# Four conv layers in one kernel: linear attention as one pipeline of 12 items, its aggregation sums in SBUF

## Chip, cores and metric

The kernel runs on one core of a Trainium2 chip. The metric is the device time of one execution in microseconds; the kernel before takes 8581.61 us, the median of three runs (8575.27 to 8585.84). Five engines work side by side, each through its own queue in order: PE (matmul), DVE (elementwise and reductions), ACT (activation and copies), POOL (here: indirect gathers) and SP (plain DMAs).

## The reference, cut to what matters

Input x is (4, 256, 64, 64) in fp32. Four layers follow, each `x = x + layer(groupnorm(x))`.

```python
# layer 0: 1x1 conv, depthwise 3x3 -> offsets and mask, deformable sampling, then SE and a 256-1024-256 feed-forward
# layer 1: linear attention
qkv = relu(conv1x1(x, qkv_w) * qkv_bn_scale + qkv_bn_bias)        # 768 channels
agg = depthwise5x5(qkv, agg_dw_w) + agg_dw_b
agg = agg * agg_pw_w + agg_pw_b                                   # per channel
t = concat([qkv, agg]).reshape(B, -1, 3 * 8, H * W)
q, k, v = split(t, 3, axis=2);  q, k = relu(q), relu(k)
vk = einsum('bhdn,bhen->bhde', v, k)
out = einsum('bhde,bhen->bhdn', vk, q)
denom = einsum('bhe,bhen->bhn', k.sum(-1), q)
out = relu(conv1x1(out / (denom + eps), proj_w) * s + b)
# layer 2: 3x3 conv with binarised weights
# layer 3: non-local attention: softmax(theta(x)^T phi(maxpool(x))) g(maxpool(x)), a 1x1 conv, + x
```

## The kernel before, in words

Each image (n = 0 to 3) goes through generators that yield a cost after each few instructions: `convolve` and `shifts` (layer 0 up to the sampling tables), `sample` (the deformable sampling), `feedforward`, `layer1`, `layer2` and `layer3`. All intermediate images lie in DRAM; blocks of 512 pixels x 256 channels are loaded again by each generator.

`run` puts generators side by side with `beside(steps, number, *works)`: for each step of the leading generator the others are advanced in proportion to their declared total cost, within a share of the stage (lo to hi). The stages are: convolve(0); sample(0) beside convolve(1 to 3) and the shifts; sample(1) beside the weights of layer 2 (`binarise`), feed(0) and linear(0); sample(2) beside feed(1), linear(1) and second(0); sample(3) beside feed(2), linear(2) and second(1); feed(3), linear(3) and second(2); second(3). Here `linear` is layer1 and `second` is layer2, then layer3. Feed has the first fifth of a stage, linear and second the rest. In the stages with `sample` the queues of PE, DVE, ACT and POOL hold the instructions in the order in which the generators issue them (`ordered`); elsewhere a scheduler orders them.

`sample` (L195 on counts rounds of 14 pixels x 9 points). A round issues four indirect DMAs on POOL (L561) that fetch 128 rows of 1 KB each into `g`, addressed by indices in `sl` in SBUF; PE multiplies them with the weights `wm` (L568) into a half of the bank `acc`, ACT copies it out (L573), PE transposes (L578), ACT spreads (L593), and per block PE projects (L601) and DVE adds (L605). `wm` is made by DVE for four rounds at a time (L552), from `con` and `sl`, both in SBUF. `g` has seven buffers, `wm` two.

`layer1` runs three passes over the image: for t = 0, 1 the tiles k and v, then the tiles q. In each pass `rows` (L727) computes two 128-channel tiles of qkv per block (L741), ACT applies scale, bias and relu, and copies the rows into padded tiles of 20 x 68 (16 rows and a border, three buffers for each of the two tiles). As soon as 16 rows and their border are there, the chunk is handed out, and `aggregate` (L759) forms the 5 x 5 depthwise sum with `depthwise` (L169): the first tap by L178 `tensor_scalar`, 24 taps by L176 `scalar_tensor_tensor`, acc = pad * w + acc, over 128 x 1024 elements each. The accumulator `agg` lies in PSUM, in one buffer of two banks; ACT then copies it to SBUF (L764), with relu for k and q. The same `depthwise`, with nine taps, is used by `offsets` in layer 0.

What comes of a chunk is put on a list, `later`, from which each `step` takes one entry: for k and v the transposes, the copy `kt` and the products into `vk` (`outer`); for q the denominators (`dens`, DVE reciprocal), per head `num`, `rden` and the multiplication (L844), and the projection (`output`). At the end of each k, v pass the list is emptied and the sums are masked (L814 to L817).

PSUM's eight banks: `agg` two, `vk`, `acc` and `dp` one each, and three that everything else shares (`mm`), handed out in turn by `ps()`.

```python
self.mm = e(tc.tile_pool(name="mm", bufs=3, space=PSUM))
...
acc = self.ps1.tile([P, 16, W], F32, name="agg", tag="agg")
```

`layer3` forms th, ph and gt from x5, then for each 128 pixels two score banks `s` (L984), the maximum on DVE (L985, L986), the exponential on ACT (L991), eight transposes (L999, L1000), the product with gt (L1004) and the division (L1005); per block a 1x1 conv (L1010), the residual (L1011, L1012) and the store.

Of the kernel before, what the change touches and what calls it, by code (L numbers as in the profile page):

```python
# [9 lines left out]
F32 = mybir.dt.float32  # L10
# [23 lines left out]
TY, TX = H + 2, W + 3  # L34
SLOPE = 0.01
# [5 lines left out]
LINEAR = 1130  # L41
SECOND = 631
# [27 lines left out]
class Net:  # L70
    def __init__(self, ctx, tc, a, out):
        self.tc, self.nc, self.a, self.out = tc, tc.nc, a, out
        e = ctx.enter_context
        self.cp = e(tc.tile_pool(name="const", bufs=1, side="left"))
        self.gp = e(tc.tile_pool(name="gather", bufs=2, side="left"))
        self.sp2 = e(tc.tile_pool(name="samp", bufs=2, side="left"))
        self.ps1 = e(tc.tile_pool(name="ps1", bufs=1, space=PSUM))
        self.mm = e(tc.tile_pool(name="mm", bufs=3, space=PSUM))
        self.dp = e(tc.tile_pool(name="scratch", bufs=1, space=DRAM))


    def ps(self, name="ps"):
        return self.mm.tile([P, 512], F32, name=name, tag="mm")
# [85 lines left out]
    def depthwise(self, acc, src, w, k, rows, cols, r0, bias=None, step=lambda cost: cost):  # L169

        nc = self.nc
        for t in range(k * k):
# [8 lines left out]
            if t % 3 == 2 or t == k * k - 1:  # L181
                yield step(3.9)

# [251 lines left out]
    def offsets(self, n, c, y, mw, bp, used):  # L435
# [3 lines left out]
        for k in range(KT):  # L439
            acc = self.ps1.tile([P, 16, W], F32, name="agg", tag="agg")  # L440
# [76 lines left out]
    def sample(self, n, ssum):  # L517
# [4 lines left out]
        nc, sp = self.nc, self.sp2  # L522
# [177 lines left out]
    def layer1(self, n, st, st2):  # L700
# [3 lines left out]
        with tc.tile_pool(name=f"la{n}", bufs=1, side="right") as sp, \  # L704
# [14 lines left out]
            later = []  # L719

            def step(cost):

                if later:
                    later.pop(0)()
                return cost

            def rows(tiles, seen):  # L727


                new = lambda c: [self.padded(bp, 1, 20, 2, c, f"pad{i}", bufs=3) for i in range(2)]  # L730
                pads = {0: new(0)}
                for b in range(NB):
                    c, h = divmod(b, 2)
                    x = self.block(bp, self.x3_d[n], b, "xr")
                    if h and c + 1 < NCH:
                        pads[c + 1] = new(c + 1)
                    got = []
                    for i, t in enumerate(tiles):
                        ps = self.ps()
                        for k in range(KT):  # L740
                            nc.tensor.matmul(ps, qw[:, k, t * P:(t + 1) * P], x[:, k], start=k == 0, stop=k == KT - 1)  # L741
                        bn = {"bias": qb[:, t:t + 1], "scale": self.vec("qkv_s", t)}
                        dst = {j: p[i][:, 0] for j, p in pads.items()}
                        if seen:
                            v = bp.tile([P, 512], F32, name="v", tag=f"v{i}")
                            added = {} if i else {"accum_out": seen[0][:, b:b + 1]}
                            nc.scalar.activation(v, ps, AF.Relu, **bn, **added)
                            self.spread(dst, rw(v), b, 2)
                            got.append(v)
                        else:  # L750
                            self.spread(dst, None, b, 2, lambda own: nc.scalar.activation(own, rw(ps), AF.Relu, **bn))  # L751
                        yield step(3)
                    if seen:
                        seen[1](b, got)
                    if b and not h:
                        yield c - 1, [p[:, 0] for p in pads.pop(c - 1)]
                yield NCH - 1, [p[:, 0] for p in pads[NCH - 1]]

            def aggregate(pd, i, name, func, **more):  # L759

                acc = self.ps1.tile([P, 16, W], F32, name="agg", tag="agg")
                yield from self.depthwise(acc, pd, self.w5[:, i], 5, 16, W, 0, bias=self.b5[:, i:i + 1], step=step)
                v = bp.tile([P, 16, W], F32, name=name, tag="ag", bufs=3)
                nc.scalar.activation(v, acc, func, **more)  # L764
                yield step(2)
                return v

            for t in range(2):
                ks = sp.tile([P, 2, NB], F32, name=f"ks{t}")
                sums = {}  # L770

                sums[0] = self.ps1.tile([P, 2, P], F32, name="vk", tag="vk")

                def outer(kind, kv, vv, first, last):

                    at = [slice(i, i + 256) for i in range(0, kv.shape[1], 256)]
                    kts = []

                    def turned(cs):
                        pt = self.ps("pt").rearrange("p (s j c) -> p s j c", s=2, j=2)  # L780
                        for j in range(2):
                            nc.tensor.transpose(pt[:, 0, j], kv[:, cs][:, j * P:(j + 1) * P], self.ident)
                            nc.tensor.transpose(pt[:, 1, j], vv[:, cs][:, j * P:(j + 1) * P], self.ident)
                        kts.append(bp.tile([P, 2, 2, P], F32, name="kt", tag="kt", bufs=4))
                        nc.scalar.copy(kts[-1], pt)

                    def added(i):
# [384 lines left out]
```

## Time and profile before

The profiled execution took 8571.0 us, 8569.0 us of it the span of the trace; the mean granted TensorE clock was 0.842.

| | busy us | share of span | instructions |
|---|---|---|---|
| PE | 6457.6 | 75% | 35252 |
| DVE | 5259.4 | 61% | 6319 |
| ACT | 2008.5 | 23% | 4711 |
| POOL | 4583.8 | 53% | 4694 |

The costliest groups are the gathers (L561, 4688 of 978 ns) and the aggregation taps (L176, 2560 of 1288 ns). The chain that ended last is mostly PE (25% of the span) and DVE (12%). POOL works until 6594 us and not at all after. A busy share is a mean over stages with different limits, so the stages have to be looked at one by one; and idle time of an engine that doesn't set the end costs nothing.

### The profile page before, as it was taken

Reading aid. Unit: us, or ns where it says so; the run is one execution under the profiler, and the core shown is the slowest. Engines: PE = TensorE matmul, PEld = TensorE weight load, DVE = VectorE, ACT = ScalarE, POOL = GpSimd, SP = SyncE. Lnnn points to the kernel's source line nnn. Section 1 sums busy time; section 2 is a strip of 40 time slices with the busy share of each in tenths; the row PEclk is TensorE's granted clock in tenths of the full one; section 3 lists DMA queues with packets and bytes.
Section 4 is the critical chain, followed back from the end, with each engine's and each line's share of the span. In section 5 each row is a group of like instructions: output and inputs, shape, how many; then the busy total and the mean of one; then the engine's idle time right before and its main releaser. Section 6 shows DMA issues by size and latency. Waiting matters only on the chain. (4 is left out here: it accounts for less than half of the span.)

```text
span 8569.0 us, 92678 instructions
## 1 busy us (share of the span) xinstructions
PE 6457.6 (75%) x35252; PEld 3474.4 (41%) x35252; DVE 5259.4 (61%) x6319; ACT 2008.5 (23%) x4711; POOL 4583.8 (53%) x4694
## 2 busy tenths in 40 slices
PE   4666666587666668999667789896678988567887
PEld 2333433344333323444444444444444444343445
DVE  5555554635878782378877723878776278988113
ACT  1111111122221122222232222223322221222113
POOL 1777777777777776777775567777654000000000
PEclk8676767798666789999888999997888999788999
DMA  6475655565444445555443354544432211110210
GB/s 172 141 197 150 179 167 160 158 189 164 123 122 119 140 127 151 148 146 148 147 128 108 113 166 147 151 140 149 126 112 86 93 60 37 47 37 35 58 58 30
DMA packets 819964, 1054.93 MB, mean 123 GB/s; under 512 B 464320, under 2 KB 524864, under 8 KB 817984
## 3 DMA queue, kind: packets, MB, share of 16 engines
q0 software_dynamic: 225024, 614.77, 24.5%
q1 hardware_dynamic: 594496, 434.25, 17.4%
q8 instruction: 279, 4.57, 0.2%
q14 instruction: 165, 1.35, 0.0%
HBM read 880.72 MB, written 167.90 MB: 122 GB/s over the span
## 5 line engine op out<-in xcount | busy, mean ns | idle before, releaser
L561 POOL DMA_INDIRECT g<-tab,sl x4688 | 4583.1, 978 | 2010.6 <-issue 1484.2
L176 DVE SCALAR_TENSOR_TENSOR agg<-pad,vec,agg 128x1024 f32<-128x1024 f32 x2560 | 3296.0, 1288 | 69.7
L568 PE MATMUL acc<-g,wm 128*32 128x128 f32 x18752 | 1330.8, 320 | 1210.5 <-ACT at L573 628.7
L568 PEld LDWEIGHTS acc<-g,wm 128*32 128x32 f32 x18752 | 644.8, 121 | 1938.1 <-DMA g<-tab,sl 835.7
L905 PE MATMUL ps<-xp,w 128*128 128x512 f32 x2304 | 1066.3, 610 | 81.7 <-DVE xp L889 53.1
L593 ACT COPY dT<-dp 64x112 f32<-64x112 f32 x1176 | 286.6, 244 | 1627.6 <-PE dp L578 1132.6
L905 PEld LDWEIGHTS ps<-xp,w 128*128 128x128 f32 x2304 | 427.7, 193 | 568.7 <-issue 537.1
L552 DVE TENSOR_TENSOR wm<-con,sl 128x1024 f32<-128x1024 f32 (+1 forms) x296 | 358.3, 1211 | 358.6 <-PE acc L568 339.6
L686 PE MATMUL ps<-x2f,f 128*128 128x512 f32 x1024 | 476.6, 615 | 4.0 <-ACT f L677 4.0
L693 PE MATMUL ps<-hm,f 128*128 128x512 f32 x1024 | 453.6, 597 | 0.0
L167 DVE SCALAR_TENSOR_TENSOR hm<-ps,vec,lk 128x512 f32<-128x512 f32 x256 | 192.3, 751 | 417.3 <-ACT lk L166 416.2
L741 PE MATMUL ps<-xr,qw 128*128 128x512 f32 x768 | 417.6, 674 | 9.7 <-ACT pad L751 1.7
L999 PE MATMUL pt<-ident,pe 128*128 128x128 f32 x1024 | 194.2, 339 | 228.6 <-ACT pe L991 226.6
L991 ACT ACTIVATE pe<-s,mx 128x512 f32<-128x512 f32 x256 | 173.6, 683 | 714.3 <-DVE mx L986 714.3
L573 ACT COPY at<-acc 128x256 f32<-128x256 f32 (+1 forms) x588 | 218.3, 371 | 481.4 <-PE acc L568 471.8
L1004 PE MATMUL ps<-gt,pT 128*128 128x128 f32 x2048 | 320.5, 321 | 4.9 <-ACT pT L1000 2.8
L1004 PEld LDWEIGHTS ps<-gt,pT 128*128 128x128 f32 x2048 | 298.6, 231 | 50.4 <-issue 19.0
L601 PE MATMUL po<-dT,ow 128*128 128x224 f32 (+1 forms) x1216 | 293.6, 392 | 19.7 <-DVE yb L605 12.9
L166 ACT ACTIVATE lk<-ps,low 128x512 f32<-128x512 f32 x256 | 175.9, 687 | 557.0 <-PE ps L686 557.0
L694 DVE TENSOR_TENSOR xyf<-xyf,ps 128x512 f32<-128x512 f32 x64 | 44.0, 688 | 409.6 <-PE ps L693 409.6
L686 PEld LDWEIGHTS ps<-x2f,f 128*128 128x128 f32 x1024 | 192.0, 194 | 232.8 <-issue 222.4
L693 PEld LDWEIGHTS ps<-hm,f 128*128 128x128 f32 x1024 | 190.6, 190 | 231.5 <-issue 231.1
(226 smaller groups left out, 7037.4 us busy)
## 6 DMA issues: line engine op xcount, KB each, us to landing
x<-x SPq DMA_DIRECT2D x160, 512.0 KB
g<-tab,sl POOLq DMA_INDIRECT x4688
xr<-x SPq DMA_DIRECT2D x96, 512.0 KB
x<-in_x SPq DMA_DIRECT2D x64, 512.0 KB
tab<-xo SPq DMA_DIRECT2D x512, 64.0 KB
y<-yc SPq DMA_DIRECT2D x32, 512.0 KB
x2f<-x SPq DMA_DIRECT2D x32, 512.0 KB
xyf<-x SPq DMA_DIRECT2D x32, 512.0 KB
```

The source lines that it names most:

```text
L176: nc.vector.scalar_tensor_tensor(acc, s, wt, acc, ALU.mult, ALU.add)
L552: nc.vector.tensor_tensor(wm[:, 0:nu], self.con("own").unsqueeze(1).unsqueeze(1).to_broadcast(sh), sl[:, r:r + nu, G:].unsqueeze(3).to_bro ...
L561: nc.gpsimd.indirect_dma_start(out=g[:, i, :], out_offset=None, in_=table, in_offset=bass.IndirectOffsetOnAxis(ap=sl.bitcast(I32)[:, r, i: ...
L568: nc.tensor.matmul(acc[32 * i:32 * i + 32, :], wm[:, r4, 4 * i + 2 * x:4 * i + 2 * x + 2, :], g[:, i, x * P:(x + 1) * P], start=x == 0, st ...
L573: nc.scalar.copy(at[u].rearrange("p v c -> p (v c)")[:, 0:nu * P], acc[:, 0:nu * P])
L593: nc.scalar.copy(dT[b][hs, :, q0:q0 + m * (v1 - v0)].rearrange("p g (v o) -> p g v o", o=m), dp[u][hs, v0:v1, :, s, 0:m].rearrange("p v g ...
L601: nc.tensor.matmul(po[m][:, 0:np_], self.ow[:, k, m * P:(m + 1) * P], dT[b][:, k, 0:np_], start=k == 0, stop=k == G - 1)
L686: nc.tensor.matmul(ps, f1[:, k, m * P:(m + 1) * P], x2[:, k], start=k == 0, stop=k == KT - 1)
L693: nc.tensor.matmul(ps, f2[:, k, m * P:(m + 1) * P], hm[:, k], start=k == 0, stop=k == 4 * KT - 1)
L741: nc.tensor.matmul(ps, qw[:, k, t * P:(t + 1) * P], x[:, k], start=k == 0, stop=k == KT - 1)
L905: nc.tensor.matmul(ps, w[:, k, t, m * P:(m + 1) * P], xp[:, k, t // 3:t // 3 + 8, t % 3:t % 3 + W], start=i == 0, stop=i == KT * 9 - 1)
L1004: nc.tensor.matmul(ps[:, 0:P], pT[:, m], gt[:, m], start=m == 0, stop=m == 7)
```

## The change

- *Aggregation sums.* `aggregate` and `offsets` accumulate in SBUF tiles (`ag`, four buffers; `agg`, two). For k and q the relu becomes an entry of `later` that works in place; v isn't copied any more. The two PSUM banks go to the shared pool, five banks instead of three.
- *One pipeline.* `rows` runs through all three passes as one generator, without a drain between them. A chunk of two tiles is an item, 3 passes x 4 chunks. While an item is aggregated, its steps 12, 14, 16 and 18 (`LEADS`) each advance `rows` by one tile, so the next item is ready when the first is done. `vk` holds the sums of both t in one bank. The masked sums (`summed`) are an entry of `later`. The declared cost falls from 1130 to 930.
- *The tail.* The pools of `sample` are closed before it. feed(3) and linear(3) run beside layer2(2) alone; then layer2(3) beside layer3(2); then layer3(3). In linear(3) (`alone`) the banks `acc` and `dp` join the shared ones, the tiles get one more buffer, and every third tile is aggregated by `products`: ACT forms each tap's product, POOL adds it. In the last two stages layer3 takes `acc`, `dp` and `vk` for its scores (`wide`).
- *Small.* The statistics tiles and `ssum` move to the constant pool; in layer3 the x5 tile shares a buffer with `pT`, and the residual has a tile of its own, `r5`, with one buffer.

```diff
+LEADS = 12, 14, 16, 18
...
-LINEAR = 1130
-SECOND = 631
+LINEAR = 930
+CONV, SECOND = NB * 32 + 2, 631
...
-        self.mm = e(tc.tile_pool(name="mm", bufs=3, space=PSUM))
+        self.mm = e(tc.tile_pool(name="mm", bufs=5, space=PSUM))
+        self.banks, self.alone = cycle(["mm"]), False
...
     def ps(self, name="ps"):
-        return self.mm.tile([P, 512], F32, name=name, tag="mm")
+        tag = next(self.banks)
+        return (self.mm if tag == "mm" else self.ps1).tile([P, 512], F32, name=name, tag=tag)
...
+    def products(self, pool, acc, src, w, k, rows, cols, r0, bias, step):
+        nc = self.nc
+        for t in range(k * k):
+            s = src[:, r0 + t // k:r0 + t // k + rows, t % k:t % k + cols]
+            if t:
+                m = pool.tile([P, rows, cols], F32, name="m", tag="product", bufs=4)
+                nc.scalar.activation(m, s, AF.Copy, scale=w[:, t:t + 1])
+                nc.gpsimd.tensor_tensor(acc, acc, m, ALU.add)
+            else:
+                nc.scalar.activation(acc, s, AF.Identity, bias=bias, scale=w[:, t:t + 1])
+            if t % 3 == 2 or t == k * k - 1:
+                yield step(0.5)
...
-            acc = self.ps1.tile([P, 16, W], F32, name="agg", tag="agg")
+            acc = bp.tile([P, 16, W], F32, name="agg")
...
-            def step(cost):
+            def step(cost, chains=False):
+                nonlocal count
                 if later:
                     later.pop(0)()
+                if chains:
+                    count += 1
+                    if count in LEADS:
+                        next(made, None)
                 return cost
...
-            def aggregate(pd, i, name, func, **more):
-                acc = self.ps1.tile([P, 16, W], F32, name="agg", tag="agg")
-                yield from self.depthwise(acc, pd, self.w5[:, i], 5, 16, W, 0, bias=self.b5[:, i:i + 1], step=step)
-                v = bp.tile([P, 16, W], F32, name=name, tag="ag", bufs=3)
-                nc.scalar.activation(v, acc, func, **more)
-                yield step(2)
-                return v
+            def aggregate(pd, i, name, relu=True, **more):
+                nonlocal turn
+                turn += 1
+                acc = bp.tile([P, 16, W], F32, name=name, tag="ag", bufs=room(4))
+                tick = lambda cost: step(cost, True)
+                if self.alone and turn % 3 == 2:
+                    yield from self.products(bp, acc, pd, self.w5[:, i], 5, 16, W, 0, self.b5[:, i:i + 1], tick)
+                else:
+                    yield from self.depthwise(acc, pd, self.w5[:, i], 5, 16, W, 0, bias=self.b5[:, i:i + 1], step=tick)
+                if relu:
+                    later.append(lambda: nc.scalar.activation(acc, acc, AF.Relu, **more))
+                return acc
...
+            made = rows()
+            for _ in range(3 * NCH):
+                while not ready:
+                    next(made)
+                    yield step(3)
+                t, tiles, c, pd = ready.pop(0)
+                count, got = 0, []
+                for i, m in enumerate(tiles):
+                    more = {} if t == 2 or i else {"accum_out": ks[t][:, 1, c:c + 1]}
+                    got.append((yield from aggregate(pd[i], m, ("ak", "av")[i], t == 2 or not i, **more)))
+                if t == 2:
+                    output(c, pd, got)
                     continue
+                outer(t, 1, *map(fl, got), False, c == NCH - 1)
+                if c == NCH - 1:
+                    later.append(partial(summed, t))
...
-                x = self.block(bp, self.x5_d[n], b, "x5")
+                x = self.block(bp, self.x5_d[n], b, "x5", tag="pT")
...
-                    s = [self.ps("s") for _ in range(2)]
+                    if not wide:
+                        s = [self.ps("s") for _ in range(2)]
+                    elif j % 2:
+                        s = [self.ps1.tile([P, 512], F32, name="s", tag="vk"), self.ps("s")]
+                    else:
+                        s = [self.ps1.tile([P, 512], F32, name="s", tag=tag) for tag in ("acc", "dp")]
...
-                r = self.block(bp, self.x5_d[n], b, "x5")
+                r = self.block(bp, self.x5_d[n], b, "r5", bufs=1)
...
-        beside(range(64), 64, *behind(N - 1), (second(N - 2), SECOND, 0.2, 1))
-        for _ in second(N - 1):
+        self.banks, self.alone = cycle(["mm", "mm", "acc", "mm", "mm", "dp", "mm"]), True
+        beside(range(64), 64, *behind(N - 1), (conv(N - 2), CONV, 0.2, 1))
+        self.banks = cycle(["mm"] * 5)
+        beside(range(64), 64, (conv(N - 1, "right"), CONV, 0, 1), (pooled(N - 2, True), SECOND - CONV, 0, 1))
+        for _ in pooled(N - 1, True):
             pass
```

In the diff `pooled` is layer3 and `conv` is layer2; `room(bufs)` is bufs plus one in the tail.

## The prediction

> **What bounds the kernel now.** I read the page's busy shares first (no engine above 75%, so no average decides), then cut the span into stages with the table by windows. Columns: stretch, its length, then busy time with count of PE, PEld, DVE, ACT and POOL, then the granted clock, the DMA share and GB/s.
>
> ```profile
> 184.70:1707.00 1522.30, 985.13 (x6342) 551.76 (x6342) 798.16 (x1059) 248.92 (x692) 1157.70 (x1172) 0.70 0.59 166
> 1707.00:3236.00 1529.00, 1102.26 (x6746) 546.91 (x6746) 1036.06 (x1016) 343.44 (x856) 1151.15 (x1173) 0.77 0.47 140
> 3236.00:4902.00 1666.00, 1343.40 (x8397) 729.22 (x8397) 1099.53 (x1274) 456.09 (x1102) 1137.06 (x1172) 0.91 0.46 137
> 4902.00:6595.00 1693.00, 1371.01 (x8478) 747.97 (x8477) 1105.18 (x1288) 463.30 (x1116) 1137.11 (x1172) 0.90 0.47 137
> ...
> 6652.00:6895.00 243.00, 224.64 (x527) 100.23 (x527) 73.74 (x120) 49.48 (x72) 0.00 (x0) 0.96 0.24 79
> 6895.00:8006.00 1111.00, 826.75 (x2670) 454.37 (x2670) 923.64 (x1066) 278.81 (x529) 0.00 (x0) 0.86 0.14 44
> 8006.00:8262.00 256.00, 250.15 (x576) 109.70 (x576) 22.43 (x50) 14.52 (x16) 0.00 (x0) 0.98 0.19 51
> 8262.00:8569.00 307.00, 226.23 (x1040) 160.08 (x1040) 97.70 (x255) 107.78 (x232) 0.00 (x0) 0.92 0.13 45
> ```
>
> Stages S1 to S4 are sample(0) to sample(3). Each issues 1172 gathers on POOL, and a gather without delay takes 0.946 us and 0.304 us of issue, 1.25 us; 1172 of them are 1465 us. So POOL bounds S1 and S2 nearly alone. In S3 and S4 it also waits for others:
>
> ```profile
> POOL g L561 <- issue: 317.6, 1041, 0.6
> POOL g L561 <- PE acc L568: 195.8, 80, 10.3
> ```
>
> That is S3's table of waits (total us, times, longest). The same row in S2 has 26.4 us. Most of the excess falls into the last fifth of S3 and S4, where outputs of layer1 run beside the attention of layer3.
>
> The tail has no gathers: feed(3) 243 us with PE full, linear(3) beside second(2) 1111 us with DVE busy 924 us, conv(3) 256 us with PE full, layer3(3) alone 307 us with PE busy 226 us, waiting on a chain PE, DVE, ACT, PE.
>
> The view that carries the forecast is the timeline of S2, instruction by instruction (start, us, engine, line, count, idle before).
>
> ```profile
> 2301.04 13.21 DVE L176 SCALAR_TENSOR_TENSOR agg<-pad,vec,agg 128x1024 f32<-128x1024 f32 x10
> 2302.24 0.95 POOL L561 DMA_INDIRECT g<-tab,sl  x1 [0.30 <-issue]
> 2303.49 0.94 POOL L561 DMA_INDIRECT g<-tab,sl  x1 [0.30 <-issue]
> ...
> 2318.21 1.23 DVE L552 TENSOR_TENSOR wm<-con,sl 128x1024 f32<-128x1024 f32 x1 [1.34 <-PE acc L568]
> 2318.50 1.76 POOL L561 DMA_INDIRECT g<-tab,sl  x1 [0.31 <-issue]
> ```
>
> Beside ten L176 in a row, whose accumulator lies in PSUM (one input from SBUF), the gathers keep 0.95 us. The gather that starts during L552, whose two inputs both lie in SBUF, takes 1.76 us: it ends at 2320.26, 0.82 us after L552's end at 2319.44. Over all 296 L552 of the trace, a gather that starts while one runs ends 818 ns after it; one that starts first is not delayed. L362, also with two SBUF inputs, gives 819 ns. The delay summed over all L552 is 131 us (296 x 0.44 us), most of the 151 us that gathers spend above 948 ns in the whole trace. So a DVE instruction with two SBUF inputs shuts POOL out until it ends.
>
> [...] L269 (128x768) takes 0.55 us, the two-input L270 0.96 us. [...] no POOL arithmetic of this size is in the trace.
>
> **The change part by part.**
>
> ```profile
> L561 POOL DMA_INDIRECT g<-tab,sl x4688 | 4583.1, 978 | 2010.6 <-issue 1484.2 <-PE acc L568 457.8 <-DMA g<-tab,sl 39.9
> L176 DVE SCALAR_TENSOR_TENSOR agg<-pad,vec,agg 128x1024 f32<-128x1024 f32 x2560 | 3296.0, 1288 | 69.7
> L167 DVE SCALAR_TENSOR_TENSOR hm<-ps,vec,lk 128x512 f32<-128x512 f32 x256 | 192.3, 751 | 417.3 <-ACT lk L166 416.2
> L362 DVE SCALAR_TENSOR_TENSOR x<-yc,vec,x 128x512 f32<-128x512 f32 x64 | 47.6, 744 | 7.1 <-PE cv L336 6.5
> ```
>
> *Aggregation sums in SBUF.* L362 (all SBUF) against L167 (PSUM in) says 7 ns less, so the 2560 L176 go from 1.288 to about 1.28 us. They follow each other after 35 ns: a period of 1.315 us. [...] DVE is not the bound in S1 to S4, so this is worth almost nothing there. The cost is on POOL: every L176 now has two SBUF inputs. Within a row of L176 the gather falls into step: after a delay its next start comes 0.818 + 0.304 us after the instruction's end and its read 0.128 us later (946 - 818 ns), 1.25 us in all, before the next L176 ends at 1.315. So each gather loses 0.06 us instead of half an instruction. At a row's start the phase is arbitrary; there I take the 0.44 us of L552. Rows of back-to-back L176, counted in the trace: 60 in S1, 98 in S2, 137 in each of S3 and S4. S1: 60 x 0.44 + 240 x 0.06 = 41 us; S2: 98 x 0.44 + 576 x 0.06 = 78; S3, S4: 137 x 0.44 + 35 = 95 each. A row often starts just behind an L552 whose delay is already in the time; I take 35, 65, 80, 80. Bounds: 0 (all rows merge, phase kept) and twice that (every row's start costs a full instruction).
>
> *Five banks, relu moved, rows made ahead.* Before, two of three shared banks are held by `s` until DVE's max and ACT's exp; PE stands before other matmuls, the gathers' among them, and POOL behind it. Five banks and a relu issued a step later (L764 held ACT for 418 us in the whole trace waiting for L176) remove part of S3's and S4's 196 us of POOL waits. But ACT's exp still stands behind DVE (147 us between 6000 and 6594), and DVE's load there, above 90% at POOL's free rate, hardly changes. I take 65 us in each, from 20 to 140. S3 and S4: 80 - 65 = +15 each. The qkv matmuls, `xr` loads on SP and pad copies are the same in number and only issued earlier, in steps 12 to 18 of an item, behind that item's work: nothing. S1 to S4: 35 + 65 + 15 + 15 = +130.
>
> *Linear(3) beside conv(2).* Of 24 sums 8 go to ACT and POOL: 200 products on ACT at about 1.24 us (L893, 640 columns, 0.916; L1011, 512 columns, 0.808; extended) are 248 us beside ACT's 279 of 1111 us, hidden[...]. DVE keeps 16 x 24 = 384 L176 at 1.315, 505 us, 16 L178 at 0.75, 12 us, and some 90 us that read PSUM or one input. If POOL's add and L176 exclude each other, as L552 and the gather do, the stretch is their sum: [...] plus 30 us for the first rows and last outputs: 980. All 24 sums on DVE would be 24 x 32.3 = 775 us plus 90, so the offload costs more than it saves. ACT's queue holds relu, kt and pad copies behind products that wait for a product buffer (four), so whatever slows POOL also slows pads. The stretch no longer carries layer3(2), nor its 98 us of DVE work.
>
> *Conv(3) beside layer3(2), then layer3(3) with wide banks.* Conv takes PE 250 us, layer3 192 us at full rate (from chain pieces: 32 matmuls of 512 columns in 13.73 us, 16 of 128 in 2.05): 442, with gaps 490. Layer3 alone, its scores in four further banks: 32 rounds of 5.3 us of PE are 170, with its first part of 40 us and gaps 245, against 307 now.
>
> *Sum of the tail:* 980 + 490 + 245 = 1715 against 1111 + 256 + 307 = 1674: +41. Feed(3) stays PE-bound. With +130 the profiled execution's 8571 becomes 8742; the runs' median lies 10 us above that execution, so 8750.
>
> **The rivals.**
> *B, the adds run beside DVE* (faster). POOL and DVE interleave below whole instructions. Then DVE's 505 + 12 + 90 = 607 us sets the stretch, 650 with gaps, 330 less: 8420. Place: from linear(3)'s first item to its last; decisive from the point where the stretch stays under 810 us (980 - 171, the whole loss). For it: the gather's own read doesn't lengthen L552 (1.22 us whether one falls into it or not). Against: L552 holds POOL for its whole length. Chance 0.17.
> *C, banks win in S3 and S4:* relief 140 instead of 65 in each, tail as forecast: 8600. For it: S2, without layer3, has only 26 us of such waits. Against: ACT's exp behind DVE. Chance 0.13.
> *D, the tail jams:* ACT behind products behind POOL delays pads and conv's inputs (L893), the stretch takes 1200: 8970. For it: ACT is in order. Against: ACT is three quarters idle there. Chance 0.10.
> That the rows are not really made ahead can't be: the order of PE's instructions shows them between the items.
>
> **How the numbers follow.** A has 0.60, own range 8640 to 8880 (gather cost from 0.4 to 1.7 times, relief 20 to 110, stretch 930 to 1050). Low end 8450: it leaves out most of B's lower half; high end 8900 leaves out D's upper part and a little of A: together 0.2. This kernel's measurement can't tell less than 0.2% from none. Faster: B 0.17, C and A 0.04: 0.21. Same 0.05. Slower 0.74.
>
> **What would show it.** Right: gathers' mean up from 978 to about 1025 ns, with ends 0.82 us after an aggregation instruction; POOL's waits for PE in S3 and S4 near 130 us; POOL adds and L176 alternating, one or the other stretched to 3 us or more, linear(3) near 980 us; layer3(3) near 245. Wrong: gathers at 978 ns (no exclusion by the scalar_tensor_tensor), [...] or S3 and S4 near 1530 us (C).

## The result and the profile after

The changed kernel takes 8689.6 us (median of 4 runs, 8684.3 to 8692.35), the kernel before 8578.44 us beside it: a ratio of 1.013, interval 1.0112 to 1.0148. It is 1.3% slower. The profiled execution's span is 8682.5 us against 8569.0, so 113.5 us are to be found. Line numbers have moved: the 24 taps of a sum are L178 now (L176 before), its first tap L180, the gathers L577 and their matmuls L584. As in the prediction, the tail is what follows the last gather.

The table by windows of the changed kernel shows S1 to S4, feed(3), the stretch of linear(3) and conv(2), conv(3) beside layer3(2), and layer3(3) alone. Columns are those of the prediction's table.

```profile
188.00:1755.00 1567.00, 1001.70 (x6342) 558.10 (x6342) 781.67 (x1059) 249.87 (x692) 1206.45 (x1172) 0.69 0.58 162
1755.00:3327.00 1572.00, 1164.57 (x6849) 577.52 (x6850) 1024.07 (x1026) 340.62 (x859) 1210.93 (x1173) 0.78 0.47 136
3327.00:4928.00 1601.00, 1343.21 (x8308) 731.56 (x8307) 1078.02 (x1267) 447.22 (x1084) 1208.19 (x1172) 0.92 0.49 142
4928.00:6567.00 1639.00, 1372.63 (x8486) 747.41 (x8487) 1088.88 (x1290) 457.55 (x1108) 1211.53 (x1173) 0.92 0.49 142
6608.00:6845.00 237.00, 226.91 (x536) 102.66 (x536) 70.20 (x104) 50.34 (x75) 0.00 (x0) 0.96 0.23 72
6845.00:8015.00 1170.00, 625.48 (x1641) 292.29 (x1641) 886.01 (x643) 386.46 (x492) 668.28 (x192) 0.75 0.11 34
8015.00:8453.00 438.00, 430.22 (x1617) 252.49 (x1616) 121.65 (x305) 117.05 (x247) 0.00 (x0) 0.99 0.20 60
8453.00:8682.50 229.50, 194.79 (x1036) 144.70 (x1036) 92.63 (x243) 101.03 (x231) 0.00 (x0) 0.98 0.15 49
```

S1 and S2 are 45 and 43 us longer than before, S3 and S4 65 and 54 us shorter; together 31 us are gained. The loss is in the tail. From feed(3)'s last matmul to conv(3)'s first it was 1122 us before (the prediction's 1111 and 11 us of edges). It is 1170 now, though layer3(2) has left this stretch. Then come 438 + 229.5 us where there were 558. From the last gather to the end the tail takes 2116 us against 1974.

The 1170 us hold more than linear(3). Its last instruction ends at 7935 us, and the last 80 us belong to conv(2): PE is busy for 74.6 of them, DVE for 11.4 and POOL not at all. Before, conv(2) was done long before linear(3) ended.

*The gathers.* The group of the gathers in the changed kernel (count, busy us, mean ns, idle us before):

```profile
L577 POOL DMA_INDIRECT g<-tab,sl x4688 | 4837.1, 1032 | 1728.0 <-issue 1313.3
```

The mean rose from 978 to 1032 ns: 4688 times 54 ns are 253 us. The idle time before gathers fell by 283 us, from 2010.6 to 1728.0. The two nearly cancel. The timeline of S2 shows how a gather gets longer (start, us, engine, line, count, idle before):

```profile
2323.85 9.28 DVE L178 SCALAR_TENSOR_TENSOR ak<-pad,vec,ak 128x1024 f32<-128x1024 f32 x7
...
2328.97 1.02 POOL L577 DMA_INDIRECT g<-tab,sl  x1 [0.30 <-issue]
2330.29 1.02 POOL L577 DMA_INDIRECT g<-tab,sl  x1 [0.30 <-issue]
2331.61 1.01 POOL L577 DMA_INDIRECT g<-tab,sl  x1 [0.30 <-issue]
...
2340.23 5.25 DVE L178 SCALAR_TENSOR_TENSOR av<-pad,vec,av 128x1024 f32<-128x1024 f32 x4
...
2340.62 1.72 POOL L577 DMA_INDIRECT g<-tab,sl  x1 [0.30 <-issue]
```

Inside a row of taps the gathers run in step with DVE: 1.02 us each, one every 1.32 us instead of 1.25. The gather that meets the beginning of a new row (2340.23) takes 1.72 us, about as the one beside L552 did before. Over the whole trace 2002 gathers start while a tap L178 runs, and they end 0.82 us after it (median; 0.818 to 0.875 for eight in ten).

POOL's waits for PE in S3, 195.8 us before, have fallen to a quarter; in S4 they fell from 223.8 to 86.1 us:

```profile
POOL g L577 <- PE acc L584: 48.3, 41, 4.2
```

*The tail.* The timeline of the changed kernel in linear(3):

```profile
6979.13 31.57 POOL L194 TENSOR_TENSOR ak<-ak,m 128x1024 f32<-128x1024 f32 x4 [20.53 <-ACT m L193]
...
6996.68 1.28 DVE L178 SCALAR_TENSOR_TENSOR ak<-pad,vec,ak 128x1024 f32<-128x1024 f32 x1
6997.88 1.28 DVE L178 SCALAR_TENSOR_TENSOR av<-pad,vec,av 128x1024 f32<-128x1024 f32 x1
6999.07 2.83 DVE L180 TENSOR_SCALAR av<-pad,vec,b 128x1024 f32<-128x1024 f32 x1
7001.83 9.95 DVE L178 SCALAR_TENSOR_TENSOR av<-pad,vec,av 128x1024 f32<-128x1024 f32 x3
```

Up to 6998 us two sums alternate on DVE (ak, av), their taps follow every 1.195 us without a gap, and POOL's add waits: the first of the four adds lasts 22.2 us. Then only one sum runs, and DVE and POOL alternate: three taps take 9.95 us, 3.3 us each, and the last three adds 3.1 us each on average. Two sums don't always keep the add out: from 7544 to 7621 us ak and av alternate too, but their taps start every 3.2 us on average, and 24 adds run beside them in 78.6 us. Over all 192 adds the shortest takes 2.34 us, the median 3.20, the longest 26.9.

The table of waits for the stretch (us, times, longest) shows who stands behind the adds:

```profile
ACT m L193 <- POOL av L194: 180.6, 76, 24.9
ACT m L193 <- POOL ak L194: 164.9, 74, 16.0
PEld pt L812 <- ACT ak L801: 134.1, 5, 52.3
```

ACT's products wait 345 us for POOL, because there are four product buffers; the relu of a finished sum (L801) stands behind them, and PE waits up to 52 us for that relu. DVE waits for pads too:

```profile
DVE ak L180 <- ACT pad L445: 58.4, 4, 18.5
```

### The profile page after: what moved, and what is told of

Same layout as the page of the kernel before. It is cut to its first block, busy times and chain, and to the rows that moved or that the text cites. A ratio compares the mean times of both kernels' runs of the same rounds, so it can differ in the third digit from the quotient of the medians.

```text
span 8682.5 us, 93037 instructions
## 1 busy us (share of the span) xinstructions
PE 6476.2 (75%) x35252; PEld 3473.8 (40%) x35252; DVE 5242.0 (60%) x6119; ACT 2193.8 (25%) x4879; POOL 5506.1 (63%) x4886
## 5 line engine op out<-in xcount | busy, mean ns | idle before, releaser
L577 POOL DMA_INDIRECT g<-tab,sl x4688 | 4837.1, 1032 | 1728.0 <-issue 1313.3
L584 PE MATMUL acc<-g,wm 128*32 128x128 f32 x18752 | 1391.9, 320 | 1288.0 <-DMA g<-tab,sl 720.3
L178 DVE SCALAR_TENSOR_TENSOR ak<-pad,vec,ak 128x1024 f32<-128x1024 f32 x1056 | 1539.4, 1460 | 30.1 <-ACT pad L449 4.1
L584 PEld LDWEIGHTS acc<-g,wm 128*32 128x32 f32 x18752 | 668.2, 120 | 2070.2 <-DMA g<-tab,sl 1022.7
L178 DVE SCALAR_TENSOR_TENSOR av<-pad,vec,av 128x1024 f32<-128x1024 f32 x1056 | 1461.9, 1389 | 25.0
L194 POOL TENSOR_TENSOR av<-av,m 128x1024 f32<-128x1024 f32 x96 | 339.1, 3532 | 369.5 <-ACT m L193 315.7
L194 POOL TENSOR_TENSOR ak<-ak,m 128x1024 f32<-128x1024 f32 x96 | 329.2, 3429 | 203.7 <-ACT m L193 196.6
L178 DVE SCALAR_TENSOR_TENSOR agg<-pad,vec,agg 128x1024 f32<-128x1024 f32 x256 | 328.2, 1283 | 7.5
L815 ACT COPY kt<-pt 128x512 f32<-128x512 f32 x256 | 147.5, 585 | 638.2 <-PE pt L813 635.7
L193 ACT ACTIVATE m<-pad,vec 128x1024 f32<-128x1024 f32 x192 | 220.3, 1158 | 345.5 <-POOL av L194 180.6
L1037 PEld LDWEIGHTS ps<-gt,pT 128*128 128x128 f32 x2048 | 266.5, 206 | 59.0 <-issue 40.6
```

Source lines behind the costliest of these rows:

```text
L178: nc.vector.scalar_tensor_tensor(acc, s, wt, acc, ALU.mult, ALU.add)
L193: nc.scalar.activation(m, s, AF.Copy, scale=w[:, t:t + 1])
L194: nc.gpsimd.tensor_tensor(acc, acc, m, ALU.add)
L577: nc.gpsimd.indirect_dma_start(out=g[:, i, :], out_offset=None, in_=table, in_offset=bass.IndirectOffsetOnAxis(ap=sl.bitcast(I32)[:, r, i: ...
L584: nc.tensor.matmul(acc[32 * i:32 * i + 32, :], wm[:, r4, 4 * i + 2 * x:4 * i + 2 * x + 2, :], g[:, i, x * P:(x + 1) * P], start=x == 0, st ...
L1037: nc.tensor.matmul(ps[:, 0:P], pT[:, m], gt[:, m], start=m == 0, stop=m == 7)
```

## The experiments

Two questions were open: how much of the tail's loss is exclusion between POOL's adds and DVE, and how much the order of the queues; and what brought S3 and S4 their relief. The second could not be read from one trace, because the sums' place, the number of banks, the relu's place and the rows' lead all changed together.

### First group: the tail, and a first look at the stages

e1, all 24 sums of linear(3) on DVE:

```diff
-                if self.alone and turn % 3 == 2:
+                if False:
```

> The changed kernel, but all 24 sums of linear(3) stay on DVE with their accumulator in SBUF; no products on ACT, no adds on POOL. Theory L (adds on POOL and two-SBUF-input instructions on DVE exclude each other, and this exclusion makes the tail long): 24 sums of 24 x 1.32 + 0.81 us are 780 us, with 90 us of other DVE work and 30 us of edges the stretch of linear(3) falls from 1046 to 850-920 us, and the stage after it, which carried conv(2)'s remainder, from 543 to about 500; total 8450-8560 us. Rival N (the adds are not the cause; POOL takes real work off DVE): a third of the sums comes back to DVE, 8 x 32 us = 260 us, the stretch goes to about 1250-1300 us, total about 8900 us. S1 to S4 unchanged within 10 us under both.

e2, three banks (the other two lie unused):

```diff
-        self.mm = e(tc.tile_pool(name="mm", bufs=5, space=PSUM))
+        self.mm = e(tc.tile_pool(name="mm", bufs=3, space=PSUM))
```

> The changed kernel with three common PSUM banks instead of five (two banks lie unused); all else, the sums in SBUF and the relu a step later too, as changed. Theory K (the banks bring the relief in S3 and S4): POOL's idle beyond the issue gap goes back from 37 and 71 us to about 170 and 200 us, S3 and S4 from 1600 and 1637 to about 1720-1770 each, and the tail loses some 10-40 us; total 8890-9000 us. Rival R (the relu moved by a step and the rows made ahead bring it): S3 and S4 stay within 20 us of 1600 and 1637, only the tail's 10-40 us are lost; total 8690-8750 us. S1 and S2, without layer3, unchanged within 10 us under both.

e3, sums in PSUM in S1 to S4, three banks there (offsets likewise), seven in the tail. The pool `pg` has one accumulator, and ACT copies each sum at once; the main part of the edit:

```diff
+                if not self.alone:
+                    acc = self.pg.tile([P, 16, W], F32, name="agg", tag="agg")
+                    yield from self.depthwise(acc, pd, self.w5[:, i], 5, 16, W, 0, bias=self.b5[:, i:i + 1], step=tick)
+                    v = bp.tile([P, 16, W], F32, name=name, tag="ag", bufs=room(4))
+                    nc.scalar.activation(v, acc, AF.Relu if relu else AF.Copy, **more)
+                    if relu:
+                        later.append(lambda: None)
+                    return v
```

> The changed kernel, but in S1 to S4 the sums lie in PSUM again (copied or relu'd to SBUF by ACT at the end of each sum) with three common banks; the tail as changed (sums in SBUF, seven banks, products and adds). Theory L (two SBUF inputs delay gathers): gathers beside sums go back to 0.95 us, S1 about 1521, S2 about 1527 us, 45 us less each; mean gather about 980 ns. S3 and S4: with theory K (banks bring the relief) about 1665 and 1690 us, total about 8720 us; with rival R (relu step and rows ahead bring it) about 1530-1570 us each, total 8450-8520 us; but the copy stands at once behind the sum again, as before the change, so if the relu's place is what counted, it is as with K. Rival G (gathers are late for another reason, such as the rows' loads and copies moved earlier): S1 and S2 stay at 1566 and 1570 us.

e4, the same the other way round: in the tail DVE's 16 sums in PSUM with five shared banks, POOL's 8 in SBUF; S1 to S4 as changed. The condition, beside e3's:

```diff
-                if not self.alone:
+                if self.alone and turn % 3 != 2:
```

> The changed kernel in S1 to S4; in the tail the 16 sums of DVE lie in PSUM (one input from SBUF), copied by ACT, beside the 8 sums of ACT's products and POOL's adds in SBUF; five banks in that stretch. Theory L: exclusion gone, POOL adds 2.34 us each, taps about 1.29 us, both without gaps; DVE 16 x (24 x 1.32 + 1.4) = 530 us plus 90 and some 2 us of hand-over to ACT's copy per sum, the stretch 650-780 us instead of 1046; total 8350-8450 us. Rival Q (ACT's queue sets it: pad copies, relu and kt stand behind products that wait for a product buffer): adds and taps speed up but the stretch stays at 900-1050 us, ACT's waits on POOL stay near 345 us, total 8580-8690 us.

In this group the kernel before took 9484 us, on chip 2 of the record (the second group ran on 7). There POOL idled 172 to 243 us in each of S1 and S2, in all four kernels (4 and 5 us in the changed kernel's first trace), and PE stood still with no cause that the trace shows. The table of waits of e1 from 300 to 1700 us has 97 such stops:

```profile
PE acc L584 <- issue: 253.6, 97, 27.8
```

So totals and S1 to S4 of these four can't be set against the first result. What was expected of S1 to S4 there was not met: neither e1's "unchanged within 10 us" nor e3's 45 us less in S1 and S2. Two things can be read: the tails (e2 and e3, with the changed tail, took 2115 and 2107 us against 2116), and the length of single gathers. The tails of e2 and e3 also have five and seven shared banks, so the banks hardly matter there. The kernels measured 9165 (e1, ratio 0.9676, 0.9638 to 0.9714), 9491 (e2, 1.0011, 1.0002 to 1.002), 9516 (e3, 1.0038, 1.0026 to 1.005) and 9306 us (e4, 0.9817, 0.9789 to 0.9844).

*e1.* Tail 1844 us, 272 less than changed, and 130 less than before. The stretch from feed(3)'s last matmul to conv(3)'s first by windows:

```profile
7613.00:8499.00 886.00, 598.58 (x1640) 278.99 (x1639) 800.11 (x843) 166.46 (x291) 0.00 (x0) 0.81 0.14 43
```

886 us, where the changed kernel has 1170; rival N, which had 200 us or more added, falls. The expectations of e1 and e4 count a shorter stretch, 1046 us in the changed kernel, so their 850 to 920 are not to be compared with 886. From feed(3)'s last matmul to DVE's last tap it is 1028 us in the changed kernel and 818 in e1. By either count the drop (210 or 284 us) is larger than theory L's 126 to 196. DVE has 200 instructions more than in the changed kernel (843 against 643) and is busy 86 us less. The offload makes the stretch 284 us longer. Some 61 of them are conv(2)'s remainder, which runs alone for 80 us in the changed kernel and for 18 in e1.

*e4.* The timeline of the tail:

```profile
7698.30 58.27 POOL L195 TENSOR_TENSOR av<-av,m 128x1024 f32<-128x1024 f32 x24 [347.30 <-ACT av L197]
...
7699.93 14.52 DVE L179 SCALAR_TENSOR_TENSOR agg<-pad,vec,agg 128x1024 f32<-128x1024 f32 x11
...
7748.09 0.09 DVE L435 MEMSET pad<- 128x40 f32 x1 [27.42 <-ACT m L194]
...
7855.82 0.09 DVE L435 MEMSET pad<- 128x40 f32 x1 [27.07 <-ACT m L194]
```

With DVE's sums in PSUM, 24 adds go through in 58.27 us, 2.43 us apart with a median of 2.35 in work, beside eleven taps at 1.32 us. So the exclusion is gone here. Yet the stretch falls only from 1170 to 1047 us. The last two lines say why. A POOL sum takes 58 us, a DVE sum 33; then DVE's next instruction is the memset of a pad buffer whose last reader is a product on ACT, which goes at POOL's pace. DVE stands 27 us, in order, with the taps behind it. The table of waits sums it up:

```profile
DVE pad L435 <- ACT m L194: 137.0, 5, 27.8
```

To the last tap it is 919 us, against the 1028 and 818 above. That is rival Q's range (900 to 1050 in its count); theory L's 650 to 780 was wrong. One sign of Q failed: ACT's waits for POOL were to stay near 345 us, and are 202.5. Of the 284 us that the adds cost, 123 go with the exclusion (1170 - 1047) and 161 remain (1047 - 886). The split is an estimate: e4 has costs of its own, since each PSUM sum must be copied before DVE may begin the next.

```profile
DVE agg L181 <- ACT av L800: 48.4, 7, 24.7
DVE agg L181 <- ACT ak L800: 23.0, 5, 11.1
```

So 123 is rather the least that the exclusion takes and 161 the most that is left to the held buffers and queues. Conv(2)'s remainder is among the 161: in e4 it again runs alone for 80 us.

*Gathers in e3* have a mean of 986 ns, in e1 and e2, with sums in SBUF, of 1042 and 1045: theory L's rule holds for single gathers on this chip too. The stages there don't show it: e3's gathers are 41 and 62 us shorter in sum than e2's in S1 and S2 (both with three banks), but POOL idles 34 and 63 us more, and the stages are as long (1765 and 1752 us against 1772 and 1751).

### Second group: the stages again, with the changed kernel as yardstick

f0 is the changed kernel. f1 is e1 and e2 together, f2 is e1 and e3 together. f3 has PSUM sums and three banks in S1 and S2, SBUF sums and five banks in S3 and S4, and all sums of linear(3) on DVE.

> The changed kernel itself, unaltered, as the yardstick of this chip for the other three, stage by stage. Expected: 1.011 to 1.015 of the kernel before if the chip is like that of the first comparison (before 8578 us); near 1.00 if it is like that of e1 to e4 (before 9484 us), where POOL waited some 200 us in each of S1 to S4 whatever the kernel.

> The changed kernel with three common banks for five and, in the tail, all 24 sums of linear(3) on DVE. Tail: 1844 us as in e1, or up to 40 us more if the two banks matter there. S1 to S4 against the yardstick: theory K (banks bring the relief of S3 and S4): S3 and S4 100 to 140 us longer each. Rival R (relu a step later, rows ahead): within 25 us each. e2 hinted at R (three banks 25 and 18 us longer than e1), but on a chip where PE itself paused.

> Sums of S1 to S4 in PSUM with three common banks, tail with all 24 sums on DVE in SBUF with seven banks. Theory L: gathers lose nothing beside sums, S1 and S2 each 40 to 50 us shorter than the yardstick; S3 and S4 with R 50 to 70 us shorter, with K 50 to 80 us longer than the yardstick (relief lost, gather cost saved), the copy that stands at once behind its sum included. Tail 1844 us, 272 less than changed. Total on a chip like the first: with R about 8200 us, with K about 8450 us; rival G (gathers not delayed by the sums' operands): S1 and S2 as the yardstick.

> Sums of S1 and S2 in PSUM with three banks; S3 and S4 with sums in SBUF and five banks, as changed; tail with all 24 sums on DVE. Theory L and K: S1, S2 40 to 50 us shorter than the yardstick each, S3 and S4 equal to it, tail 272 us shorter: on a chip like the first 8690 - 90 - 272 = about 8330 us, 3% less than before. With R f2 is the faster of the two by about 120 us. Rival G: 8420 us.

Here the kernel before took 8575.13 us, close to the first comparison's 8578.44. Results: f0 8685.52 us (1.0127, 1.0107 to 1.0147), f1 8415.44 (0.9811, 0.9794 to 0.9828), f2 8237.49 (0.9603, 0.9586 to 0.962), f3 8282.39 (0.9659, 0.9641 to 0.9677).

The next table is worked out from the traces. A stage is measured from its first gather's start to its last one's. "Gather excess" sums what gathers last above 0.948 us; "idle" sums POOL's gaps between gathers above the 0.304 us of issue. The row "before" is from the first comparison's trace. The changed kernel's two traces, the first and f0, differ by up to 4 us in a stage.

| kernel | S1 | S2 | S3 | S4 | gather excess S1-S4 | idle S1-S4 | tail |
|---|---|---|---|---|---|---|---|
| before | 1521 | 1527 | 1665 | 1692 | 50, 43, 29, 29 | 9, 21, 173, 200 | 1974 |
| f0 (changed) | 1566 | 1566 | 1604 | 1637 | 97, 95, 104, 104 | 6, 6, 35, 69 | 2120 |
| f1 (three banks) | 1563 | 1574 | 1616 | 1644 | 93, 101, 115, 108 | 6, 8, 36, 71 | 1830 |
| f2 (PSUM, three banks) | 1524 | 1516 | 1576 | 1613 | 51, 42, 35, 34 | 9, 9, 77, 115 | 1817 |
| f3 (mix) | 1521 | 1512 | 1604 | 1633 | 48, 43, 105, 101 | 9, 6, 35, 68 | 1812 |

Three readings follow. With the sums in PSUM the gather excess returns to that of the kernel before in every stage (f2), and only in S1 and S2 where only these are changed (f3): the delay goes with the sums' place, and rival G falls. Its size is 46, 53, 69 and 70 us (f0 less f2). Second, three banks instead of five cost 12 and 7 us in S3 and S4, and nothing in POOL's idle time: theory K falls. POOL's waits for PE in S3 of f1:

```profile
POOL g L577 <- PE acc L584: 47.4, 40, 4.3
```

Third, f2 keeps most of the relief with three banks, and is the fastest: 338 us less than before. It gives up about 42 us of POOL's waits in S3 against f0 and gains 69 on the gathers. Its gathers and its waits in S3:

```profile
L577 POOL DMA_INDIRECT g<-tab,sl x4688 | 4598.4, 981 | 1820.0 <-issue 1311.9
```

```profile
POOL g L577 <- PE acc L584: 93.2, 57, 4.9
```

f3 was expected at 8330 and f2, if R held, at 8200: both in the expected order, and within 50 us. But S3 and S4 of f2 are only 28 and 24 us shorter than f0's, where R had 50 to 70, and f2's lead over f3 is 45 us, not 120: part of the relief does go when the sums return to PSUM.

### Third group: what brings the relief, and the adds once more

g1 makes the rows between the items instead of ahead, after everything on `later` has been issued (on e1). g2 issues the relu at once (on e1):

```diff
-LEADS = 12, 14, 16, 18
+LEADS = ()
...
                 while not ready:
+                    while later:
+                        yield step(0.01)
                     next(made)
```

```diff
                 if relu:
-                    later.append(lambda: nc.scalar.activation(acc, acc, AF.Relu, **more))
+                    nc.scalar.activation(acc, acc, AF.Relu, **more)
+                    later.append(lambda: None)
```

> The changed kernel with all 24 sums of linear(3) on DVE (as e1), and layer1's rows no longer made ahead: qkv matmuls, relus and pad copies are issued between the items, after what was put off has been issued, instead of at steps 12 to 18 of the item before. Five banks, sums in SBUF. Theory A (rows ahead bring most of the relief in S3 and S4, about 90 of 138 us): POOL's idle beyond the issue gap goes from 35 and 69 us to about 125 and 160, S3 and S4 from 1604 and 1637 to about 1690 and 1725 us. Rival (a relu issued a step later brings it all): S3 and S4 within 25 us of 1604 and 1637. S1 unchanged (it has no layer1). The tail, where DVE then waits for pads at each of 12 items, 50 to 150 us longer than e1's 1844.

> The changed kernel with all 24 sums of linear(3) on DVE, and the relu of a sum issued at once behind it instead of a step later; rows ahead, five banks, sums in SBUF. Theory A (the relu's place brings about 40 us): POOL's idle from 35 and 69 to about 75 and 110 us, S3 and S4 from 1604 and 1637 to about 1645 and 1680. Rival (the 42 us that PSUM sums with three banks had more come from the banks or the copies, not from the relu's place): S3 and S4 within 12 us of 1604 and 1637. Tail within 20 us of 1812 to 1844.

g2: 8395.84 us (0.9784, 0.9766 to 0.9801). S3 and S4 are 1606 and 1634, idle 34 and 64 us: the same as f0 within 5 us. The relu's place brings nothing where the sums lie in SBUF, as the rival said. POOL's waits in its S3:

```profile
POOL g L577 <- PE acc L584: 47.1, 45, 4.3
```

g1: 9034.5 us (1.0529, 1.051 to 1.0548), S3 and S4 1788 and 1814, more than either theory had. Some 150 us of each lie in the first tenth of the stage (302 and 325 us), where work of the stage before was still being issued: LINEAR, the number by which layer1 is spread over its stage, seems no longer to match the steps. Of the 128 matmuls of layer1's output projection (`ps<-ot,pw`) 64 fall into the stage after; in f0's S3 there are 9 of them. So g1 doesn't separate the theories, and h1 repeats the trial on f2 with LINEAR at 1130. Its edits beside f2's:

```diff
-LINEAR = 930
+LINEAR = 1130
...
-LEADS = 12, 14, 16, 18
+LEADS = ()
...
                 while not ready:
+                    while len(later) > 4:
+                        yield step(0.01)
                     next(made)
```

> f2 (sums of S1 to S4 in PSUM, three banks, all 24 sums of linear(3) on DVE) with the rows made between the items and not ahead, the work put off issued until four pieces are left, and LINEAR at 1130 as in the kernel before, so that no part of linear(n) spills over the end of its stage as it did in g1 (first tenth of S3 and S4 302 and 325 us). Theory A (rows ahead bring the relief): S3 and S4 go from f2's 1576 and 1613 to about 1665 and 1692 us as in the kernel before, POOL's idle from 77 and 115 to about 170 and 200 us, most of it in the last fifth. Rival B (the new order of layer1's sums as a whole, not the rows' place): S3 and S4 within 25 us of 1576 and 1613. Tail 40 to 150 us longer than f2's 1817, since DVE waits for pads at 12 items. Total with A about 8450-8550, with B 8290-8400 us.

h1: 8802.69 us (1.0266, 1.0248 to 1.0285). S1 to S4 are 1521, 1628, 1799 and 1800 us, POOL's idle 9, 119, 304 and 304 us. POOL's waits in S3, beside f2's 93.2 us above and the 195.8 of before:

```profile
POOL g L577 <- PE acc L584: 328.6, 82, 41.8
```

Against f2, POOL's idle rises by 227 us in S3 and 189 in S4. Rival B had S3 and S4 within 25 us of f2's, so its numbers fall, and the direction is theory A's. But the size is not: h1 lies 134 us above the kernel before in S3, and has waits of up to 41.8 us where before had 10.3. And three things changed together, the rows' place, LINEAR, and `later`, which is now emptied in bursts down to four entries. The bursts put put-off work on PE at once, ahead of the gathers' matmuls: the eighth and ninth tenth of S3 take 220 and 265 us (151 and 179 in f2), and 32 and 64 of the 128 matmuls of layer1's output projection fall there. So h1 is not the old order. It shows that the order of layer1's pieces can cost more than the whole relief, and not that the rows' place brought it.

The traces tell where the 96 us between before and f2 in S3 lie. In the first tenth POOL idles 22 us before and 1.5 in f2; there before still issues 23 such matmuls of the image ahead, f2 only 9. In the last two tenths it idles 111 us before and 57 in f2. Beside the rows' place, f2 keeps the missing drains, the new LINEAR and the small edits in layer3 (`x5`, `r5`), and none of these was undone alone.

In the tail the stretch grows from about 887 us to 992 in g1 and 966 in h1.

g3 tries the adds again, on f2: in the tail every second of three sums goes to POOL, its products spread over the two DVE sums beside it, which lie in PSUM, with five banks; the rows are led by six steps of such a round. The heart of the edit:

```diff
+                    for s, pd, m, name, relu, more in todo:
+                        for cost in aggregate(pd, m, name, relu, got, s, **more):
+                            if count % 2:
+                                next(adds, None)
+                            yield cost
```

> As f2 (S1 to S4 with sums in PSUM and three banks), but in the tail POOL adds again: every second of three sums, its products and adds spread over the two sums of DVE beside it, which lie in PSUM and are copied by ACT; five banks in that stretch. e4 had the adds undisturbed, but DVE idle for 27 us per POOL sum behind pads and products on ACT. Theory Q (ACT's order was what was left): with the products spread, eight rounds of 66 to 75 us are 530-600 us, plus 90-120 us at the edges: the stretch 640-740 us instead of 887, total 8040-8130 us. Rival (ACT's queue still holds copies and pads behind products that wait for POOL): 850-1050 us, total 8200-8400 us.

g3: 8337.96 us (0.9722, 0.9704 to 0.9739), 100 us more than f2; the stretch is 996 us, not 640 to 740. The adds run undisturbed (median 2.35 us), but DVE waits as in e4:

```profile
DVE pad L434 <- ACT m L193: 84.0, 5, 27.0
DVE agg L180 <- ACT av L799: 46.0, 7, 30.7
```

The first is again the pad held by products, the second the copy of a PSUM sum that stands in ACT's queue before the next sum can begin. The rival holds. More pad buffers were not tried.

## Why the prediction was right, and where it was wrong

The side held, and so did two of the mechanisms, the delay of the gathers and the exclusion of POOL's adds. The time was 60 us too high (8750 against 8689.6), and that closeness is luck: two errors nearly cancel. S1 to S4 were forecast at +130 us and came out at -31, the tail at +41 and came out at +157 (1837.5 us from feed(3)'s last matmul to the end, against 1680). The end of the sampling and feed(3), forecast unchanged, are 16 us shorter.

*The gather rule* held. Forecast gross costs of 35, 65, 80 and 80 us stand against 46, 53, 69 and 70 from f0 and f2: 260 against 238 in sum. Lock-step at 1.32 us, 1.02 us per gather and a longer gather at a row's start are in the timeline; the mean of 1025 ns came out at 1032, and the ends lie 0.82 us after a tap's. (The delay beside L552 sums to 122 us in the trace rather than 131; nothing hangs on it.)

*The step that failed in S1 to S4* is the term "I take 65 us in each" for five banks and the relu, together with "The qkv matmuls, `xr` loads on SP and pad copies are the same in number and only issued earlier ...: nothing". POOL's waits for PE were to be near 130 us in S3 and S4; they are 48.3 and 86.1. The relief is 136 and 129 us of idle time by the first trace (138 and 131 by f0), twice the term and at the upper end of its range of 20 to 140. The banks bring none of it (f1), the relu's place none (g2). Of S3's 138 us, 96 stay when the sums go back to PSUM with three banks (f2), of S4's 131 us 85: these come from the rest of the change, the new order and pace of layer1 and the small edits in layer3, which were priced at nothing or not at all. Which of them counts stays open, since h1 changed too much to tell. The other 42 and 46 us go with the sums' move to SBUF. For them the chain of cause was not tried apart; what PSUM sums have besides is the copy on ACT that must be done before the next sum may begin. The prediction counted moved work instruction by instruction and found the same number; it did not ask what then stands in PE's queue ahead of the gathers' matmuls. The size of the relief is rival C's (140 against 65), its cause is not.

*The step that failed in the tail* is "If POOL's add and L176 exclude each other ... the stretch is their sum: ... 980". In the measure used here, to conv(3)'s first matmul, that is 991 us; it was 1170. The exclusion is there as forecast: POOL's adds and taps alternate. The price per add in the forecast sum was shown by no trace; in the changed kernel the shortest of the 192 adds takes 2.34 us, and a first tap from SBUF to SBUF, priced at 0.75 us, 0.81 (L180, median). With these the sum is 505 us of taps, 449 of adds, 13 of first taps and 30 of edges, 997 us, or 1008 to conv(3)'s first matmul, so the prices aren't what failed. What the sum lacked is waiting in queues, which the prediction had named itself and given to rival D: "whatever slows POOL also slows pads". e4 takes the exclusion away and up to 161 us of loss stay. The sum also took conv(2) to be hidden beside linear(3), and its last 80 us were not; why they are left over in the changed kernel and in e4, and hardly in e1, no run shows. D's stretch of 1200 was the better estimate. The sentence "ACT is three quarters idle there" was no argument: here an ACT that was busy for a third of the stretch (386 of 1170 us) still held the relu and the pads that stood behind a waiting product.

Taps whose two inputs lie in SBUF and POOL's adds hold each other up: the median add takes 3.20 us in the changed kernel and 2.35 in e4, where the sums of the taps lie in PSUM. The same taps delay the gathers, as L552, a tensor_tensor, did before: the gathers' mean is 1032 ns in the changed kernel and 981 in f2, with these sums in PSUM.

*Conv(3) beside layer3(2) and layer3(3)* were sized at 490 and 245 us; they took 438 and 229.5. Both were terms of the sum a little too large: PE is busy 430 of the 438 us, so the gaps allowed for on top of 442 us of PE work did not occur.

*Rival B* fell with the trace of the changed kernel. e4 and g3 show its adds at 2.35 us beside undisturbed taps, with sums in PSUM, but even then the stretch stays far from its 650 us (1047 and 996).

## What to carry to other kernels

Before an accumulator moves from PSUM to SBUF, list what POOL does meanwhile: in these traces a DVE instruction with two SBUF inputs (L552, L362, L178) held back a gather that started beside it until 0.82 us after its own end. An offload to a slower engine must be judged by what it holds (buffers, and the in-order queues behind them), not by its engine's idle share: here 8 sums less on DVE made the stretch 284 us longer. And when several edits share one stage, undo them one at a time before naming the one that helped: the two that looked like the cause (banks, relu) moved none of POOL's idle time, and most of the relief (96 of 138 us in S3) stayed with edits that had been given no price. Undo the edit and nothing else, its pacing included: g1 and h1 changed more than the rows' place, and so could not name it.

## What was not expected of the hardware

In linear(3) of the changed kernel the taps of two independent chains on DVE started every 1.195 us without a gap in some stretches, and POOL's add beside them took up to 26.9 us. In others two chains and the adds took turns (taps every 3.2 us from 7544 to 7621 us), as one chain and the adds do (three taps of 3.3 us each beside adds of 3.1); a chain alone has a tap every 1.32 us. What decides between the two is not shown by a run. On the chip of the first group of experiments PE paused for up to 27.8 us ahead of a matmul (e1) without a visible cause; the kernel before took 9484 us there against 8578, and e2's ratio was 1.0011, where the changed kernel's (five banks) is 1.013 elsewhere. There e3's gathers were 41 and 62 us shorter than e2's in S1 and S2, and POOL idled 34 and 63 us more: the stages were as long.
